# Written slots for the experts' steps, and early rows for the second place of every other block, in a graph attention and experts kernel

## The chip, the cores and the metric

The kernel runs on one core of a Trainium2 chip, in one launch. The time is the device time of that core in microseconds (us), as the median of several runs. A profile is one further execution, recorded by the hardware profiler.

## What is computed

A layer of a graph network and a feed-forward layer with experts, in float32. There are 30,000 nodes with 256 features and 510,000 edges, sorted by destination, each of one of 8 types. For each of the 8 types and 4 heads a node has a vector of 64 features:

```python
feat_all = jnp.einsum('ni,rhid->rnhd', inputs, conv_weights)      # inputs: layernorm(x)
feat_src_e = feat_all[edge_type, edge_src]
feat_dst_e = feat_all[edge_type, edge_dst]
el = jnp.sum(feat_src_e * attn_l[edge_type], axis=-1)
er = jnp.sum(feat_dst_e * attn_r[edge_type], axis=-1)
e = jax.nn.leaky_relu(el + er, negative_slope=LEAKY_SLOPE)
m = jax.ops.segment_max(e, edge_dst, num_segments=N_NODES)
ex = jnp.exp(e - m[edge_dst])
denom = jax.ops.segment_sum(ex, edge_dst, num_segments=N_NODES)
alpha = ex / denom[edge_dst]
h = jax.ops.segment_sum(alpha[..., None] * feat_src_e, edge_dst, num_segments=N_NODES)
```

Then x + h + bias goes through a layernorm, and the result is added to a shared network of three layers and to the best two of four experts, weighted by a softmax of the gates.

## The kernel before

There are two main stages. (A third part, a slow path for unusual inputs, runs zero times with these.)

**Features.** The 30,000 nodes are 235 tiles of 128. For each tile TensorE computes all types and heads at once in five groups of columns (`group`, the matmuls at L305). ACT and VectorE copy the results out of PSUM (L307), and SP's queue stores 128 x 8320 bytes to `feat` in HBM (`store`, L319). `feat` has one row of 260 numbers (1040 bytes) for each node and type: 4 heads of 64 features, and each head's part of the attention. GpSimd (POOL) adds the bias to x once for each four tiles (`residual`, L274). SP's loads, the copies and the matmuls run in an order written out by hand (`manual_schedule`); each engine executes its own queue in order.

Beside the tiles run generators, one step of which is put in after the third group of a tile and later also after the fifth (`aside`): `edge_records` writes an index record for each edge, and `places` makes the plan of each of the 252 blocks. A block is 16 places of 128 edges, one edge for each partition and place. The plan brings the edge with the smallest row number of a partition into place 0, with a `mark` that remembers where it stood. `places` works on batches of 12 blocks, in VectorE instructions with some copies on POOL.

Place 0 is thereby an early row: it lies in a tile that is finished well before the end of the stage. From tile 178 on, `first_rows` gathers these 252 rows of 128 partitions from the first three quarters of `feat` (L615, on POOL) and writes them to `stage` in HBM (L610, on SP).

**Edges.** The 252 blocks (and a last one of 18 places) are pipelined by hand. An iteration t of the loop has six chunks c, in each of which several blocks at different steps put their instructions into the queues:

- `load(t + 2)` and `gather(t + 1)` at c = 0. `gather` reads the early row from `stage` (SP, L931) and the other 15 places by one indirect DMA each (POOL, L933) into `ft`, a ring of four blocks.
- `dest_select`, `dest_expand` and `dest_pick` select the destination's part of the attention with one-hot matmuls (TensorE, L987) and VectorE (L998, L1000).
- `scores(t)` at c = 1 adds both parts, and calls `exchange`, which undoes the swap of places (VectorE, L1018, L1020, L1022), since the maximum over neighbours is taken by scans over the edges in order (L1033, L1034). `turn_ends`, `across`, `turn_back` carry the maximum across partitions. `softmax(t)` at c = 5 subtracts it (L1062 to L1065) and calls `exchange` again to bring the values back to the swapped places. `exps` is on ACT (L1071, L1072).
- `weigh` multiplies the gathered rows by the weights (VectorE, L1079), six pieces a block. `onehot` (ACT, L1010, L1011) makes the one-hot matrices with which `sums` adds the rows by destination (TensorE, L1086). `finish` divides (L1104 to L1107).
- When four blocks are finished, `residual_sum` makes the 22 steps of the experts (`Experts.steps`) for these 512 nodes and appends them to the list `todo`, of which one step is taken in each chunk, so in 22 chunks one after another of the next 24. Steps are matmuls with what follows on ACT or VectorE: `turn` (L742, L744), `layer` (L798, L799), `gates` (L750), `choose`, `weigh` (L835, L838), `last` (L851 to L857). What must come after a step's matmuls, such as VectorE's sum of the output (L857) and its store (`put`, L1097), waits in `late` for the start of the next chunk.

Of the kernel before, what the change touches and what calls it, by code (L numbers as in the profile page):

```python
# [10 lines left out]
F32 = mybir.dt.float32  # L11
# [34 lines left out]
WI, WD, WA, WP, W1, WT, WR = 0, U, 2 * U, 3 * U, 4 * U + 1, 6 * U + 3, 6 * U + 3 + U * 4  # L46
# [7 lines left out]
def kernel(  # L54
# [47 lines left out]
    stage = dram.tile([NBLK * P, H * HW], F32, name="stage")  # L102
# [119 lines left out]
    with ExitStack() as cx:  # L222
# [263 lines left out]
        BT = 3 * NT // 4  # L486
        count = {"ready": 0, "sent": 0}
        low = gp.tile([P, NBLK], I32, name="low")
        lowc = gp.tile([P, NBLK], I32, name="lowc")

        def places(cl):


            GB = 12
# [28 lines left out]
            yield  # L523
            done = None
            for k, (b0, n) in enumerate(batches):
# [4 lines left out]
                key = kp.tile([P, GB, U], F32, name="key", bufs=1)[:, :n]  # L530
                km = kp.tile([P, GB], F32, name="km", bufs=1)[:, :n]
                x = rc[:, :, :U, :3].rearrange("p b u f -> p b f u")
                mark = of[:, :, WA:WA + U]
                nc.vector.scalar_tensor_tensor(key, rc[:, :, :U, 0], float(U),
                                               iu[:, None, :].to_broadcast([P, n, U]), op0=ALU.mult, op1=ALU.add)
                nc.vector.tensor_reduce(km, key, AX.X, ALU.min)
                yield
                if done:
                    done()
                nc.vector.tensor_tensor(mark, key, km[:, :, None].to_broadcast([P, n, U]), op=ALU.is_equal)  # L540
                m3 = mark[:, :, None, :].to_broadcast([P, n, 3, U])
                t3 = kp.tile([P, GB, 3, U], F32, name="t3", bufs=1)[:, :n]
                nc.vector.tensor_mul(t3, x, m3)
                yield
                for f in range(3):
                    nc.vector.copy_predicated(x[:, :, f, 1:], o[:, :, WA + 1:WA + U],
                                              x[:, :, f, 0:1].to_broadcast([P, n, U - 1]))
                yield
                with nc.allow_low_precision(reason="integers below 2 ** 24"):
                    nc.vector.tensor_reduce(x[:, :, :, 0], t3, AX.X, ALU.add)  # L550
# [52 lines left out]

        def first_rows():

            n, kept = 4, []
            fp = cl.enter_context(tc.tile_pool(name="first", bufs=3))

            def keep(b0, m, fr):
# [795 lines left out]
```

## Time and profile before

| | us |
|---|---|
| median of 3 runs | 6651.61 |
| lowest and highest | 6647.99 and 6666.63 |
| the profiled execution | 8380.65 |
| its span, first to last instruction | 8379.0 |

The profiled execution is much longer than the runs without a profile. In the page of the profile, "busy" is the time in which an engine executes an instruction; in the row of a group, `x` is the number of instructions. "Idle before" is the time that the engine stood still before such instructions, with what ended most of it. The gathers are POOL's `DMA_INDIRECT`:

| group | count | busy us, mean ns of one |
|---|---|---|
| L933, gathers of the edge stage | 3798 | 3608.6, 950 |
| L615, gathers of the early rows | 252 | 240.6, 955 |
| L1086, TensorE's sums | 8100 | 2305.4, 421 |
| L1079, weighing on VectorE | 1518 | 1289.9, 850 |

In a timeline, each row has the start, the duration, the engine, the line, the operation with its tiles and shapes, how many instructions were merged into the row, and in brackets the idle time before with what ended it ("issue": nothing that the profile shows; "remote": a signal without a recorded sender).

### The profile page before, as it was taken

Reading aid. Unit: us, or ns where it says so; the run is one execution under the profiler, and the core shown is the slowest. Engines: PE = TensorE matmul, PEld = TensorE weight load, DVE = VectorE, ACT = ScalarE, POOL = GpSimd, SP = SyncE. Lnnn points to the kernel's source line nnn. Section 1 sums busy time; section 2 is a strip of 40 time slices with the busy share of each in tenths; the row PEclk is TensorE's granted clock in tenths of the full one; section 3 lists DMA queues with packets and bytes.
Section 4 is the critical chain, followed back from the end, with each engine's and each line's share of the span. In section 5 each row is a group of like instructions: output and inputs, shape, how many; then the busy total and the mean of one; then the engine's idle time right before and its main releaser. Section 6 shows DMA issues by size and latency. Waiting matters only on the chain. (4 is left out here: it accounts for less than half of the span.)

```text
span 8379.0 us, 96556 instructions
## 1 busy us (share of the span) xinstructions
PE 6330.2 (76%) x25254; PEld 3986.0 (48%) x25255; DVE 5381.4 (64%) x13882; ACT 3416.7 (41%) x9511; POOL 4073.5 (49%) x4327
## 2 busy tenths in 40 slices
PE   9999999956666767777666667777666777777667
PEld 5555555534444444444444444444444444444444
DVE  5557774447666666666666666666666666666665
ACT  2222222224444444444444444444444444444444
POOL 1101114665555555555555555555555555555552
PEclk9999999978888888888888888888888888888888
DMA  6657778964444444444444444444444444444441
GB/s 226 229 177 238 224 243 303 341 197 123 116 117 117 118 116 119 119 121 119 117 120 117 119 116 118 118 123 118 118 116 117 118 119 118 116 119 117 115 118 55
DMA packets 761457, 1209.52 MB, mean 144 GB/s; under 512 B 241638, under 2 KB 599789, under 8 KB 730685
## 3 DMA queue, kind: packets, MB, share of 16 engines
q1 hardware_dynamic: 565453, 663.56, 24.8%
q0 software_dynamic: 194400, 539.40, 23.3%
q8 instruction: 206, 3.38, 0.2%
q14 instruction: 358, 2.93, 0.1%
q10 hardware_dynamic: 1040, 0.26, 0.0%
HBM read 818.57 MB, written 384.23 MB: 144 GB/s over the span
## 5 line engine op out<-in xcount | busy, mean ns | idle before, releaser
L933 POOL DMA_INDIRECT ft<-feat,rk x3798 | 3608.6, 950 | 2919.9 <-PE po L1086 956.0
L1086 PE MATMUL po<-ft,oh 128*128 128x260 f32 x8100 | 2305.4, 421 | 286.3 <-DVE ho L1107 149.5
L1086 PEld LDWEIGHTS po<-ft,oh 128*128 128x128 f32 x8100 | 1565.4, 208 | 569.7 <-issue 292.4
L305 PE MATMUL ps<-w,xT 128*128 128x448 f32 (+1 forms) x4700 | 1712.6, 519 | 14.3 <-DVE xT L294 8.6
L1079 DVE TENSOR_TENSOR ft<-ft,p 128x768 f32<-128x768 f32 x1518 | 1289.9, 850 | 394.8 <-issue 184.1
L1010 ACT ACTIVATE oh<-icol,rk 128x128 f32<-128x128 f32 x4032 | 1329.1, 389 | 66.4 <-remote 45.5
L305 PEld LDWEIGHTS ps<-w,xT 128*128 128x128 f32 x4700 | 877.3, 191 | 704.9 <-issue 613.5
L798 PE MATMUL ph<-xT,w 128*128 128x512 f32 (+1 forms) x512 | 372.1, 859 | 961.8 <-issue 888.7
L307 ACT COPY fo<-ps 128x448 f32<-128x448 f32 (+1 forms) x711 | 377.3, 533 | 1087.4 <-PE ps L305 912.4
L998 DVE TENSOR_TENSOR ere<-pe,rk 128x384 f32<-128x384 f32 x1008 | 553.3, 549 | 373.4 <-remote 247.9
L1011 ACT ACTIVATE oh<-oh 128x384 f32<-128x384 f32 x1518 | 740.2, 488 | 49.4
L987 PEld LDWEIGHTS <-ohT 128*128 128x128 bf16 x4050 | 393.9, 158 | 548.8 <-issue 438.1
L798 PEld LDWEIGHTS ph<-xT,w 128*128 128x128 f32 x512 | 112.3, 260 | 1112.1 <-issue 952.5
L744 ACT COPY xT<-ph 128x512 f32<-128x512 f32 (+1 forms) x128 | 73.1, 572 | 1325.3 <-remote 1299.9
L1000 DVE TENSOR_REDUCE e<-ere 128x16 f32<-128x384 f32 (+1 forms) x1012 | 561.5, 555 | 34.8
L987 PE MATMUL pe<-erp,ohT 128*128 128x96 bf16 x4050 | 442.3, 236 | 113.3 <-DVE ohT L970 73.5
L798 PE MATMUL ph<-xT,v 128*128 128x512 f32 (+1 forms) x1024 | 500.2, 613 | 2.3 <-ACT h L799 1.5
L1062 DVE TENSOR_TENSOR c<-t,rk 128x128 f32<-128x128 f32 x252 | 71.8, 285 | 618.9 <-remote 582.0
L1071 ACT ACTIVATE p<-e 128x64 f32<-128x64 f32 (+1 forms) x253 | 70.4, 278 | 844.9 <-DVE e L1022 741.8
L307 DVE COPY fo<-ps 128x448 f32<-128x448 f32 (+1 forms) x464 | 242.3, 528 | 221.9 <-PE ps L305 194.2
L1040 PE MATMUL t<-ident,fb 128*4 128x128 f32 x253 | 70.8, 280 | 383.6 <-DVE fb L1033 196.7
L851 PE MATMUL pf<-w,h 128*128 128x256 f32 x506 | 203.2, 491 | 189.1 <-ACT wT L844 85.1
(206 smaller groups left out, 7422.2 us busy)
## 6 DMA issues: line engine op xcount, KB each, us to landing
feat<-fo SPq DMA_DIRECT2D x234, 1040.0 KB
dr<-dk_d SPq DMA_DIRECT2D x252, 516.0 KB
ft<-feat,rk POOLq DMA_INDIRECT x3798
stage<-fr SPq DMA_DIRECT2D x63, 520.0 KB
ft<-stage SPq DMA_DIRECT2D x252, 130.0 KB
xt<-xb_d SPq DMA_DIRECT2D x253, 128.0 KB
out_dram<-og SPq DMA_DIRECT2D x253, 128.0 KB
xb_d<-xb SPq DMA_DIRECT2D x58, 512.0 KB
```

Source lines behind the costliest of these rows:

```text
L305: nc.tensor.matmul(ps, t["xT"][:, k, :], w[:, k, c0:c1], start=k == 0, stop=k == 1)
L307: eng(t["fo"][:, h0:h1, :HD], ps[:, :n].rearrange("p (a d) -> p a d", d=HD))
L798: nc.tensor.matmul(ps[:, :self.w], lhs, rhs, start=i == 0, stop=i == len(pairs) - 1)
L851: nc.tensor.matmul(pf[:M], self.h2[:, tok], w3, start=True, stop=False)
L933: nc.gpsimd.indirect_dma_start(out=s.ft[:, u].rearrange("p h d -> p (h d)"), out_offset=None, in_=feat[:, :], in_offset=bass.IndirectOffse ...
L987: nc.tensor.matmul(pe[:, u - u0].rearrange("p f r -> p (f r)"), s.ov[:, u, :], s.erp.rearrange("n h k r -> n (h k r)"), start=True, stop=True)
L998: nc.vector.tensor_mul(ere, s.pe[:, :u1 - u0], s.th[:, u0:u1, None, :].to_broadcast([P, u1 - u0, H * 3, R]))
L1000: nc.vector.tensor_reduce(s.e[:, :, u0:u1].rearrange("p h u -> p u h"), ere.rearrange("p u (h k) r -> p u h (k r)", h=H), AX.X, ALU.add)
L1010: nc.scalar.activation(s.oh[:, u, :], icol, AF.Abs, bias=s.nd[:, u:u + 1])
L1011: nc.scalar.activation(s.oh[:, u0:u1], s.oh[:, u0:u1], AF.Relu, bias=1.0, scale=-1.0)
L1079: nc.vector.tensor_mul(fc, fc, pc[:, :, None].to_broadcast([P, (u1 - u0) * H, HD]))
L1086: nc.tensor.matmul(s.po.rearrange("n h d -> n (h d)"), s.oh[:, u, :], s.ft[:, u].rearrange("p h d -> p (h d)"), start=u == 0, stop=u == s. ...
```

## The change

Two things change.

1. In every other block (t even) the second place, too, gets an early row: of the remaining 15 places of each partition, the one with the smallest row number is swapped into place 1. So there are 252 + 126 = 378 early rows. `places` makes both swaps, `first_rows` gathers all 378 rows during the features, from tile 156 on, and `gather` reads one or two of them from the two tensors `stages`. How far into `feat` a gather may reach now depends on when it is issued (`rows_there`). The tensors hold three blocks' rows side by side (3120 bytes a partition), and are written three at a time. In the edge stage `exchange` is called for both places of such a block.

2. The 22 steps of the experts are no longer taken one after another. They have written slots (`SLOTS`), up to slot 27 of a group that starts every 24 chunks, so that the last four lie beside the first steps of the next group.

```diff
-WI, WD, WA, WP, W1, WT, WR = 0, U, 2 * U, 3 * U, 4 * U + 1, 6 * U + 3, 6 * U + 3 + U * 4
+WI, WD, WA, WP, W1, WT, WR = 0, U, 2 * U, 4 * U, 5 * U + 1, 7 * U + 3, 7 * U + 3 + U * 4
...
-    stage = dram.tile([NBLK * P, H * HW], F32, name="stage")
+    NS = 3
+    stages = [dram.tile([-(-n // NS), P, NS * H * HW], F32, name=f"stage{i}")
+              for i, n in enumerate((NBLK, (NBLK + 1) // 2))]
...
-        BT = 3 * NT // 4
+        NF = (NBLK, (NBLK + 1) // 2)
+        FIRST = NT * 2 // 3
+        RATE = 1.02 * sum(NF) / (NT - 1 - FIRST)
+        GB = 12
...
+        def rows_there(i, b0):
+            at = b0 - b0 % GB if i == 0 else NBLK + b0 - b0 % (GB // 2)
+            return min(NT - 2, int(FIRST + at / RATE) - 2) * P * R
...
             fetch(0)
-            yield
+            for _ in range(6):
+                yield
...
-                nc.vector.scalar_tensor_tensor(key, rc[:, :, :U, 0], float(U), ...)
-                nc.vector.tensor_reduce(km, key, AX.X, ALU.min)
+                nc.gpsimd.memset(o[:, :, WA + U:WA + 2 * U], 0)
+                for i in range(2):
+                    v = rc[:, ::i + 1, i:U]
+                    m, w = (n + i) // (i + 1), U - i
+                    x = v[:, :, :, :3].rearrange("p b u f -> p b f u")
...
+                    nc.vector.scalar_tensor_tensor(key, v[:, :, :, 0], float(U),
+                                                   iu[:, None, :w].to_broadcast([P, m, w]), op0=ALU.mult, op1=ALU.add)
+                    nc.vector.tensor_reduce(km, key, AX.X, ALU.min)
...
-                nc.gpsimd.tensor_copy(low[:, b0:b0 + n], rc[:, :, 0, 0])
-                nc.gpsimd.tensor_scalar_min(lowc[:, b0:b0 + n], rc[:, :, 0, 0], float(BT * P * R - 1))
+                for i, (c0, m, v) in enumerate(((b0, n, rc[:, :, 0, 0]), (b0 // 2, (n + 1) // 2, rc[:, ::2, 1, 0]))):
+                    most = rows_there(i, c0)
+                    nc.gpsimd.tensor_scalar_add(low[i][:, c0:c0 + m], v, float(-most))
+                    nc.gpsimd.tensor_scalar_min(lowc[i][:, c0:c0 + m], v, float(most - 1))
...
+            for i, n in enumerate(NF):
+                for b0 in range(0, n, NS):
+                    m = min(NS, n - b0)
+                    fr = fp.tile([P, NS, H * HW], F32, name="fr")
+                    for b in range(m):
+                        nc.gpsimd.indirect_dma_start(
+                            out=fr[:, b], out_offset=None, in_=feat[0:rows_there(i, b0 + b), :],
+                            in_offset=bass.IndirectOffsetOnAxis(ap=lowc[i][:, b0 + b:b0 + b + 1], axis=0))
...
-                    if m >= BT + 2:
-                        fetched = min(fetched + 1.03 * NBLK / ((NT - BT - 2) * NG), 3)
+                    if m >= FIRST:
+                        fetched = min(fetched + RATE / NG, 3)
...
+        SLOTS = (0, 1, 2, 4, 5, 7, 8, 9, 10, 11, 12, 13, 14, 15, 16, 18, 19, 21, 24, 25, 26, 27)
...
+                self.early = 2 - t % 2 if self.own else 0
...
-            if s.own:
-                nc.sync.dma_start(s.ft[:, 0].rearrange("p h d -> p (h d)"), stage[t * P:(t + 1) * P, :])
-            for u in range(1 if s.own else 0, s.u):
+            for i in range(s.early):
+                b = t >> i
+                f = b % NS * H * HW
+                nc.sync.dma_start(s.ft[:, i].rearrange("p h d -> p (h d)"), stages[i][b // NS, :, f:f + H * HW])
+            for u in range(s.early, s.u):
                 nc.gpsimd.indirect_dma_start(
...
-        def exchange(s, x):
-            if not s.own:
+        def exchange(s, x, i):
+            if i >= s.early:
                 return
-            m = wk.tile([P, H, U], F32, name="m", bufs=1)
-            nc.vector.tensor_mul(m, x, s.mark[:, None, :].to_broadcast([P, H, U]))
-            at = [P, H, U - 1]
-            nc.vector.copy_predicated(x[:, :, 1:], s.marki[:, None, 1:].to_broadcast(at),
-                                      x[:, :, 0:1].to_broadcast(at))
+            m = wk.tile([P, H, U], F32, name="m", bufs=1)[:, :, i:]
+            x = x[:, :, i:]
+            mark = s.marks[:, i, None, i:]
+            nc.vector.tensor_mul(m, x, mark.bitcast(F32).to_broadcast([P, H, U - i]))
+            at = [P, H, U - 1 - i]
+            nc.vector.copy_predicated(x[:, :, 1:], mark[:, :, 1:].to_broadcast(at), x[:, :, 0:1].to_broadcast(at))
             nc.vector.tensor_reduce(x[:, :, 0], m, AX.X, ALU.add)
...
-            exchange(s, s.e)
+            exchange(s, s.e, 1)
+            exchange(s, s.e, 0)
...
             nc.vector.tensor_sub(s.e, s.e, s.f)
-            exchange(s, s.e)
+            exchange(s, s.e, 0)
+            exchange(s, s.e, 1)
...
-                todo.extend(groups.pop(q).steps())
+                first = free[0] = max((t + 2) * NCH, free[0])
+                free[0] += T * NCH
+                for i, f in zip(Experts.SLOTS, groups.pop(q).steps()):
+                    plan.setdefault(first + i, []).insert(0, f)
...
-                    if todo:
-                        after = todo.pop(0)()
+                    for f in plan.pop(t * NCH + c, ()):
+                        after = f()
                         if after:
                             late.append(after)
```

## The prediction

> **What bounds the kernel now.** I read the page first, then windows by stage, then one group of four blocks in the timeline.
>
> ```profile
> span 8379.0 us, 96556 instructions
> ...
> PE 6330.2 (76%) x25254; PEld 3986.0 (48%) x25255; DVE 5381.4 (64%) x13882; ACT 3416.7 (41%) x9511; POOL 4073.5 (49%) x4327
> ```
>
> No engine looks full, and the profiled execution (8380.65 us) is 1729 us longer than the median of 6651.61 us. The timeline says where those 1729 us sit:
>
> ```profile
> 4101.01 0.58 ACT L744 COPY xT<-ph 128x512 f32<-128x512 f32 x1 [21.73 <-remote]
> ```
>
> ACT copies a transpose that TensorE finished near 4081 us only at 4101. "Remote" means that the signal it waited for did not come with any recorded instruction; VectorE waits in the same way there. The list of waits has this one 63 times, 1299.9 us in all, once for each group of four blocks. 1729 us over 63 groups is 27 us each, so I take these late signals, and smaller ones beside them, as part of the profiled execution, and work with each engine's own durations instead of its idle time. This is a choice, and the largest uncertainty of what follows.
>
> ```profile
> 1162.00:1313.00 151.00, 151.00 (x455) 81.90 (x454) 97.70 (x267) 39.16 (x84) 20.40 (x26) 1.00 0.76 243
> 1313.00:1750.00 437.00, 429.29 (x1282) 232.43 (x1280) 189.62 (x594) 109.21 (x233) 273.13 (x266) 0.99 0.95 331
> ...
> 2500.00:8000.00 5500.00, 3877.71 (x16860) 2565.55 (x16859) 3670.57 (x9302) 2489.57 (x7178) 3024.64 (x3183) 0.85 0.42 118
> ```
>
> Columns: stretch, length, busy time of PE, PE's loads, DVE, ACT, POOL, then clock, DMA share, GB/s. Two stages: features to about 1750 us, where PE is the bound and, in the last 437 us, the DMA engines are nearly full too; then 253 blocks of edges with no engine full.
>
> ```profile
> L1104 DVE TENSOR_SCALAR den<-po x253: 154/155/165, 1851.9 to 8323.0; 128x4 f32<-128x4 f32 x127
> ```
>
> One such instruction ends each block: 6471.1 us over 252 blocks is 25.7 us a block in the profile. For the median: 6651.6 less 1750 (features), some 50 (filling the ring) and 56 (8323 to the end) leaves about 4796 us, 19.0 us a block.
>
> What fills 19.0 us? POOL first:
>
> ```profile
> 4071.14 0.95 POOL L933 DMA_INDIRECT ft<-feat,rk  x1 [0.30 <-DVE ft L1079]
> 4072.39 0.95 POOL L933 DMA_INDIRECT ft<-feat,rk  x1 [0.30 <-issue]
> ```
>
> One gather every 1.25 us, 15 a block: 18.8 us. VectorE next: 3670.57 us busy in 5500 us, which is 214.2 blocks, so 17.1 us and 43 instructions a block. But short dependent instructions leave gaps that no other work can fill:
>
> ```profile
> 4054.47 0.23 DVE L1028 SCALAR_TENSOR_TENSOR e<-e 128x64 f32<-128x64 f32 x1
> 4054.72 0.23 DVE L1018 TENSOR_TENSOR m<-e,rk 128x64 f32<-128x64 f32 x1
> 4054.99 0.23 DVE L1020 COPY_PREDICATED e<-rk,e 128x60 f32<-128x60 int32 x1
> 4055.25 0.22 DVE L1022 TENSOR_REDUCE e<-m 128x4 f32<-128x64 f32 x1
> 4055.51 0.29 DVE L1033 TENSOR_TENSOR_SCAN fb<-penf,e 128x64 f32<-128x64 f32 x1
> ```
>
> Starts lie 0.26 us apart for 0.22 to 0.23 us of work; some 20 such gaps of 0.04 us make 0.8 us. And in each block VectorE stands idle between the softmax and the first weighing, for ACT's exponential and copy:
>
> ```profile
> 4070.17 0.95 DVE L1079 TENSOR_TENSOR ft<-ft,p 128x768 f32<-128x768 f32 x1 [0.71 <-ACT ft L1072]
> ```
>
> 17.1 + 0.8 + 0.7 = 18.6 us. So POOL (18.8) and VectorE (18.6) both lie within 2% of the pace of 19.0. PE's 3877.71 us are 18.1 us a block at a clock of 0.85, so less at full clock.
>
> **What the Trainium skill says.** "Perfetto Trace Analysis", section "DMA Instruction — SWDGE (GPSIMD)": a gather's recorded end is when the descriptors are written, not when the rows land. The trace agrees: 0.95 us each, whether the DMA share is 0.42 or 1.0. So POOL's time depends on the count of gathers. The same page, "Optimizing Scalar/DVE Operations": a VectorE instruction on SBUF carries about 60 ns of access overhead, and its profiled latency about twice that; 64 elements at 0.23 us show that small instructions cost mostly overhead here. "DMA: Bandwidth & Descriptors", section "Where 436 GB/s comes from": about 358 GB/s of HBM for a core; the trace agrees, with 357 and 365 GB/s at a DMA share of 1.03 and 1.01 in stretches of the features.
>
> **The change part by part.**
>
> *Removed from POOL's edge stage:* 126 gathers (one in every other block) of 1.2535 us (0.95 + 0.30): 157.9 us. POOL's work falls to 18.2 us a block. If POOL alone sets the pace, this is all gained.
>
> *Added to VectorE's edge stage:* the blocks with two early rows call exchange twice more, once in scores and once in softmax: 3 instructions each, 0.26 us from start to start: 1.58 us a block, 199 us over 126 blocks. The tiles of 60 and 56 elements instead of 64 and 60 save a few ns. VectorE goes to 18.6 + 0.79 = 19.4 us a block on average, above today's 19.0. Nothing else of its work goes away: steps of the experts only move. Beside what can it lie? Only VectorE's waits for others: 19.0 - 18.6 = 0.4 us a block, 100 us. Waits for gathers among them vanish as POOL gets ahead; those for PE and ACT do not. Bounds: all 199 us on the path, or 99 us. The pieces are chains at fixed places (scores, before TensorE's turn of the ends; softmax, before ACT's exponentials), and the queue behind each is the weighing that TensorE's sums wait for. I take 30 us absorbed: +169 us.
>
> *The experts' slots.* The same 22 steps, in 24 to 28 slots. TensorE's four matmuls of a 512-wide layer take 1.88 us (4013.78 to 4015.66), the 16 of the gates 1.84 us. Before, the group's second block has gates, one shared layer and four expert layers: 11.2 us on top of the sums. After, that block has 9.4 us, the third about 9.2 us, the fourth hardly any, and the four last steps fall into the next group's first block. This smooths TensorE's peak, and moves VectorE's four output sums (0.42 us each) into a block without the second exchange; but it leaves TensorE's heavy third block beside VectorE's lightest. Nothing here shows either effect alone: -50 to +60 us (a quarter us a block either way); I take 0. New group's steps come ahead of the old group's last in the shared slots, with tiles of their own; the copies of x1 alternate between two buffers, so no new wait on a buffer.
>
> *The features.* 378 gathers instead of 252, from tile 156 of 235 on at 4.94 a tile, instead of from tile 178 at 4.55. POOL: a quad of tiles lasts 29.2 us (7.31 a tile) and now has 20 gathers (25.1), one residual sum (2.36) and, while the block plans are still being made, about 2.9 us of their copies: 30.3 us. That is 1 us a quad late, some 11 quads: 12 us of lag, made up by nothing. DMA: the stretch before the gathers moves 243 GB/s, plans included. 4.94 gathers a tile read and write back 133 KB each, 180 GB/s. With the plans a fifth slower that is about 414 GB/s for 44 tiles (322 us), against some 358 GB/s: 18 MB too much, 50 us of transfer; afterwards 185 + 180 = 365 GB/s lets it recover nothing. The write-back in rows of 3120 instead of 1040 bytes may spare some. SP's queue is passed by more write-backs, each waiting for its gathers, and feature stores stand behind them; six tiles of lead hide about 44 us. What is left appears as a late start of the edge stage. Bounds 0 and +50 us; I take +25. VectorE's second ordering in the plans (11 pauses a batch instead of 9) lies beside PE-bound matmuls: nothing, as VectorE is busy 98 of 151 us there. More expert weights arrive later, but far ahead of their use.
>
> *The start of the edge stage:* the ring of four blocks fills with two gathers less: -2.5 us. SP issues one more small read in every other block: nothing, it runs ahead.
>
> Sum: 169 + 0 + 25 - 2 = +192 us. On the profiled execution, 8380.65 + 192 = 8573 us; on the median, 6651.6 + 192, rounded: **6840 us**.
>
> **The rivals.**
> (B) POOL alone sets the pace, and VectorE's true need is a whole us a block below what the profile gives (its gaps stretched by the recording, as TensorE's signals were). For it: POOL's 18.8 is the larger of the two, and a ring of four blocks can keep POOL running without a pause. Against: VectorE's durations look the same in quiet and crowded stretches. Then 6651.6 - 158 + 25 + 20 (VectorE takes over in the two-row blocks) = 6540 us. The point from which it decides: VectorE below about 18 us a block before the change.
> (C) Both fall together: gain and cost cancel, 6600 to 6700 us, about 6650.
> (D) The features also stretch: the DMA excess of 50 us and POOL's lag stop TensorE as well; 6840 + 50 = 6890 us.
> That the early rows don't get fetched in time is excluded by the order of POOL's queue: of 378 gathers 7 stand behind the last residual sum, against 10 before.
>
> **How the numbers follow.** VectorE's pace (my forecast) 0.52, B 0.27, C 0.12, D 0.09. My forecast's own range is 6740 to 6910 us: 99 to 199 us of exchange, ±55 of slots and 0 to 50 of features, not all at one end. The range for all is 6515 to 6920 us, which leaves out less than half of B's lower side and a few parts of D. A measurement here can tell 0.3% (20 us) from nothing: faster takes B and a third of C (0.31), within 0.3% a third of C (0.04), slower the rest (0.65).
>
> **What would show it.** Right: in the changed profile, VectorE's busy time in the edge stage grows by about 170 us and three more of its instructions stand in a row in every other block, while POOL's gaps at L933's successor grow. Wrong: shorter total with VectorE waiting for gathers less than before; or a shorter wait at the first weighing, which would mean that the slots freed VectorE. For the features: DMA share near 1.0 from about 1165 us, and the first gather of the edge stage later than 1750 us.

## The result, and the profile after

The changed kernel takes 7131.75 us (median of 4 runs, 7127.65 to 7135.18) against 6652.67 us before: a ratio of 1.0716 (95% interval 1.0698 to 1.0735), 479 us slower. The forecast had the direction, but 192 us for the size. On two chips every run of the kernel before took 8350 to 8480 us, like the profiled execution in the prediction, and on the others about 6655 us, so each run below is compared with the kernel before on its own chip, and the runs beside 6655 us carry the argument.

The changed kernel's profiled run (7135.18 us) agrees with its median. Its page, with the busy times, the slices of PE, and three groups of instructions (busy time, mean ns, idle time before and what ended most of it):

```profile
span 7133.5 us, 97813 instructions
...
PE 6186.2 (87%) x25254; PEld 3969.0 (56%) x25255; DVE 5576.9 (78%) x14808; ACT 3428.9 (48%) x9511; POOL 4094.6 (57%) x4390
...
PE   9999999779688888888888888888888888888888
...
L972 POOL DMA_INDIRECT ft<-feat,rk x3672 | 3479.9, 948 | 1668.4 <-PE pe L1026 536.2
...
L1121 DVE TENSOR_TENSOR ft<-ft,p 128x768 f32<-128x768 f32 x1518 | 1288.6, 849 | 364.3 <-ACT ft L1114 364.3
...
L644 POOL DMA_INDIRECT fr<-feat,lowc x378 | 372.5, 985 | 297.6 <-DMA stage<-fr 185.4
```

Three things stand here. POOL idles 1668 us ahead of the edge gathers. Some 1100 us of that are the 0.30 us between any two gathers, but with 15 gathers a block (f_features below) it is 1228 us in all: POOL waits more than before, so the time of the 126 gathers it was spared is not gained. VectorE waits 364 us at the first weighing (L1121) for ScalarE's copy: 1.44 us a block, where 0.71 us was the wait seen before. And the PE row dips in its eighth and ninth slices (about 1250 to 1600 us), inside the features, where TensorE was full before.

Where the two stages stand, by single lines (L972 is the edge gather, L933 before; L1147 ends a block, L1104 before):

```profile
L972 POOL DMA_INDIRECT ft<-feat,rk x3672: 940/946/1132, 1890.2 to 7022.5; - x194
```

```profile
L1147 DVE TENSOR_SCALAR den<-po x253: 152/154/163, 1939.8 to 7074.8; 128x4 f32<-128x4 f32 x127
```

The edge gathers of x_exch2, a run below with the features of before:

```profile
L936 POOL DMA_INDIRECT ft<-feat,rk x3798: 940/946/1197, 1742.8 to 6681.1; - x200
```

The first edge gather comes at 1890.2 us. In the runs that leave the features alone (x_exch2, s_slots2, b_hot2) it comes at 1742.8, 1744.4 and 1742.2: the features lost 147 us. The blocks then run at (7074.8 - 1939.8) / 252 = 20.38 us. f_features below, which has the old edge stage, runs at 19.10 us; 1.28 us times 252 is 323 us. 147 + 323 = 470 of the 479 us.

**The features.** Windows of the changed kernel, then of x_exch2 (columns as in the prediction):

```profile
1200.00:1300.00 100.00, 82.12 (x232) 43.36 (x230) 52.82 (x140) 18.32 (x41) 55.22 (x64) 0.91 0.85 276
1300.00:1400.00 100.00, 79.42 (x223) 42.36 (x224) 59.25 (x158) 19.19 (x42) 59.65 (x65) 0.86 0.82 262
1400.00:1500.00 100.00, 62.70 (x173) 32.58 (x172) 44.60 (x109) 14.38 (x32) 59.84 (x70) 0.81 0.84 280
1500.00:1600.00 100.00, 73.06 (x208) 38.94 (x207) 37.88 (x119) 17.35 (x37) 57.05 (x62) 0.86 1.00 305
1600.00:1700.00 100.00, 100.00 (x303) 54.55 (x302) 47.64 (x144) 25.99 (x55) 61.92 (x62) 1.00 0.92 327
```

```profile
1300.00:1400.00 100.00, 100.00 (x302) 54.28 (x301) 49.62 (x144) 26.01 (x56) 52.81 (x51) 1.00 0.88 301
1400.00:1500.00 100.00, 100.00 (x301) 54.29 (x300) 42.91 (x137) 25.70 (x54) 67.36 (x67) 1.00 1.01 359
```

From 1200 to 1600 us TensorE loses 103 us. Up to 1500 us no engine fills that hole: VectorE is about half idle, POOL is busy 55 to 60%, the DMA share is 0.82 to 0.85, and from 1300 us on the DMA engines move less than in x_exch2. That is a queue standing behind something, not a full resource; only from 1500 to 1600 us, at a DMA share of 1.00, do the windows leave it open. The changed kernel's timeline shows one such stop:

```profile
1419.84 0.95 POOL L644 DMA_INDIRECT fr<-feat,lowc  x1 [0.30 <-DMA stage<-fr]
1420.79 0.36 POOL L594 COPY rko<-a1k 128x204 f32<-128x204 f32 x1
1421.10 0.35 POOL L595 COPY rko<-a2k 128x204 f32<-128x204 f32 x1
1421.49 0.96 DVE L601 TENSOR_TENSOR rko<-rcb,it 128x768 bf16<-128x768 int32 x1 [21.68 <-POOL rko L595]
1422.36 0.42 DVE L297 COPY xT<-ptr 128x256 f32<-128x256 f32 x1
...
1422.83 1.86 PE L308 MATMUL ps<-w,xT 128*128 128x448 f32 x2 [16.37 <-DVE xT L297]
```

Read it from below. TensorE waits 16.37 us for the transposed rows xT. VectorE's copy of them stands in its queue behind L601, the last step of a plan, which has waited 21.68 us for POOL's two copies into the same tile, and those stand behind gathers in POOL's queue. The Trainium skill, "TensorE: Matmul & The Clock Gate", section "Architectural detail: the array is 16× 32×32, not 1× 128×128", gives VectorE's queue as strictly first in, first out, and GpSimdE's too for each of its cores; the trace agrees, since a copy of 0.42 us waited behind an instruction that it has nothing to do with. The gathers themselves stand still as well: 185 us in all, until earlier rows are copied out of their buffers (L644 above).

The last step of the plans and the early gathers, before (L579, L615) and in the changed kernel (L601, L644):

```profile
L579 DVE TENSOR_TENSOR rko<-rcb,it x42: 944/951/2981, 604.1 to 1264.8; 128x768 bf16<-128x768 int32 x42
```

```profile
L615 POOL DMA_INDIRECT fr<-feat,lowc x252: 943/949/1190, 1313.2 to 1731.3; - x126
```

```profile
L601 DVE TENSOR_TENSOR rko<-rcb,it x42: 941/950/959, 618.3 to 1540.7; 128x768 bf16<-128x768 int32 x42
```

```profile
L644 POOL DMA_INDIRECT fr<-feat,lowc x378: 940/946/1682, 1142.7 to 1874.3; - x189
```

Before, the gathers begin when the plans are through. Now they begin at 1143 us, and the plans run until 1541 us. The change has moved both ends: the gathers start 170 us earlier, and each of the 21 batches of plans has eleven pauses in place of nine. At the old pace of a pause the plans would end near 1426 us (618 + 661 x 11/9, an estimate from these lines).

**The edges.** ScalarE's queue in a third block of a group in the changed kernel, with VectorE's last instruction of the exchange (L1062) and the weighing that waits:

```profile
4017.38 0.69 ACT L860 ACTIVATE a<-ph,c 128x512 f32<-128x512 f32 x1
4017.96 0.61 ACT L864 COPY wide<-wt 128x512 f32<-128x512 f32 x1
4018.18 0.22 DVE L1062 TENSOR_REDUCE e<-m 128x4 f32<-128x64 f32 x1
4018.47 0.99 ACT L1049 ACTIVATE oh<-icol,rk 128x128 f32<-128x128 f32 x3
4019.49 0.53 ACT L1050 ACTIVATE oh<-oh 128x384 f32<-128x384 f32 x1
4019.92 0.27 ACT L1113 ACTIVATE p<-e 128x64 f32<-128x64 f32 x1
4020.22 0.28 ACT L1114 COPY ft<-p 128x64 f32<-128x64 f32 x1
...
4020.54 0.95 DVE L1121 TENSOR_TENSOR ft<-ft,p 128x768 f32<-128x768 f32 x1 [2.13 <-ACT ft L1114]
```

The scores e are ready at 4018.40 (4018.18 + 0.22), but the exponential (L1113) starts at 4019.92: ScalarE is still at the one-hots of the block's fifth chunk, and these came late because slot 16 has put the second half of experts2 (L860, L864) into that chunk. In the old list the 17th step lay there, the second weigh of a group, which has no ScalarE instruction. The group's first block waits as long, for another step:

```profile
4057.43 0.58 ACT L779 COPY xT<-ph 128x512 f32<-128x512 f32 x1 [6.80 <-PE ph L777]
4057.91 0.98 ACT L1049 ACTIVATE oh<-icol,rk 128x128 f32<-128x128 f32 x3
4058.93 0.53 ACT L1050 ACTIVATE oh<-oh 128x384 f32<-128x384 f32 x1
4059.48 1.28 ACT L1113 ACT_TABLE_LOAD   x1
4060.77 0.28 ACT L1113 ACTIVATE p<-e 128x64 f32<-128x64 f32 x1
```

Slot 4 is the first turn; its copy (L779) waits for TensorE, the one-hots follow, and behind them the exponential needs a table load of 1.28 us, because the group's square root came between. L1121 waits 2.22 us there. In f_features the same load is done (4076.57 to 4077.85 us in its profile) before the scores are ready (4078.17).

VectorE's account of four consecutive blocks makes the edge stage comparable. It is taken from the timelines, from one end of a block to the next, as a mean over 55 groups of four; idle is the sum of gaps over 0.1 us between VectorE's instructions:

```
kernel         work, us   idle, us   four blocks, us
f_features       71.75       4.72        76.46   (the old edge stage)
x_exch2          74.76       3.76        78.51
s_slots2         71.60       6.91        78.49
changed          74.67       7.12        81.78
k_hot            74.82       4.48        79.31
b_slothot        71.71       3.82        75.53
b_hot2           71.93       6.85        78.79
```

There are 63 groups. The change adds 2.9 us of work and 2.4 us of idle time to each.

### The profile page after: what moved, and what is told of

Same layout as the page of the kernel before. It is cut to its first block, busy times and chain, and to the rows that moved or that the text cites. A ratio compares the mean times of both kernels' runs of the same rounds, so it can differ in the third digit from the quotient of the medians.

```text
span 7133.5 us, 97813 instructions
## 1 busy us (share of the span) xinstructions
PE 6186.2 (87%) x25254; PEld 3969.0 (56%) x25255; DVE 5576.9 (78%) x14808; ACT 3428.9 (48%) x9511; POOL 4094.6 (57%) x4390
## 5 line engine op out<-in xcount | busy, mean ns | idle before, releaser
L972 POOL DMA_INDIRECT ft<-feat,rk x3672 | 3479.9, 948 | 1668.4 <-PE pe L1026 536.2
L1128 PE MATMUL po<-ft,oh 128*128 128x260 f32 x8100 | 2372.8, 431 | 400.9 <-DVE ho L1150 213.5
L1128 PEld LDWEIGHTS po<-ft,oh 128*128 128x128 f32 x8100 | 1588.6, 211 | 820.2 <-ACT ends L994 398.3
L308 PE MATMUL ps<-w,xT 128*128 128x448 f32 (+1 forms) x4700 | 1730.8, 524 | 107.0 <-DVE xT L297 104.8
L1121 DVE TENSOR_TENSOR ft<-ft,p 128x768 f32<-128x768 f32 x1518 | 1288.6, 849 | 364.3 <-ACT ft L1114 364.3
L644 POOL DMA_INDIRECT fr<-feat,lowc x378 | 372.5, 985 | 297.6 <-DMA stage<-fr 185.4
L1026 PE MATMUL pe<-erp,ohT 128*128 128x96 bf16 x4050 | 424.9, 230 | 52.8 <-DVE ohT L1009 52.1
L834 ACT ACTIVATE h<-ph,b 128x512 f32<-128x512 f32 x192 | 130.9, 682 | 449.3 <-PE ph L833 446.5
L297 DVE COPY xT<-ptr 128x256 f32<-128x256 f32 x229 | 97.2, 424 | 319.1 <-PE ptr L295 318.1
L1009 DVE TENSOR_SCALAR ohT<-dr,rowid 128x2064 bf16<-128x2064 int16 (+1 forms) x253 | 324.0, 1281 | 18.4 <-DMA feat<-fo 18.4
L833 PE MATMUL ph<-xT,w 128*128 128x512 f32 (+1 forms) x512 | 311.7, 744 | 0.2 <-ACT xT L779 0.2
L779 ACT COPY xT<-ph 128x512 f32<-128x512 f32 (+1 forms) x128 | 74.6, 584 | 462.1 <-PE ph L777 462.1
```

Source lines behind the costliest of these rows:

```text
L308: nc.tensor.matmul(ps, t["xT"][:, k, :], w[:, k, c0:c1], start=k == 0, stop=k == 1)
L644: nc.gpsimd.indirect_dma_start(out=fr[:, b], out_offset=None, in_=feat[0:rows_there(i, b0 + b), :], in_offset=bass.IndirectOffsetOnAxis(ap ...
L833: nc.tensor.matmul(ps[:, :self.w], lhs, rhs, start=i == 0, stop=i == len(pairs) - 1)
L972: nc.gpsimd.indirect_dma_start(out=s.ft[:, u].rearrange("p h d -> p (h d)"), out_offset=None, in_=feat[:, :], in_offset=bass.IndirectOffse ...
L1026: nc.tensor.matmul(pe[:, u - u0].rearrange("p f r -> p (f r)"), s.ov[:, u, :], s.erp.rearrange("n h k r -> n (h k r)"), start=True, stop=True)
L1121: nc.vector.tensor_mul(fc, fc, pc[:, :, None].to_broadcast([P, (u1 - u0) * H, HD]))
```

## The experiments

Part by part first. The first four runs were made on a chip where the kernel before takes 8370.42 us.

**The slots alone** on the kernel before (the part of the diff with SLOTS, plan and free).

> The kernel before with only the written slots for the experts' steps; the early rows and the features stay as they were. The whole change costs 479 us, of which the two profiles put 140 us before the first gather of the edge stage (1750.5 against 1890.2 us) and so 339 us into the edge stage. Theory 1 (VectorE sets the edge stage's pace, the second exchange costs its full 199 us): the slots cost the rest, 140 us, so about 6790 us. Theory 2 (POOL set the pace; exchange and saved gathers cancel; the slots are what costs): 339 us, about 6990 us. A third value, at or below 6650 us, would mean that the slots help and that the second row costs more than it shows. The late signals at the copy of the transposes, 1299.9 us in the profile before, should be gone from this profile if the slots removed them.

Measured: 8307.89 us, ratio 0.9928 (0.9909 to 0.9947). In its profile ACT's waits of 21 us at the copy of the transposes are gone, but VectorE stands still for 870 us in all at the gates (L766, 64 times), mostly for TensorE: with the new order the long waits are at another step.

**Everything but the slots:** the changed kernel with the old list of steps.

```diff
-                for i, f in zip(Experts.SLOTS, groups.pop(q).steps()):
-                    plan.setdefault(first + i, []).insert(0, f)
+                todo.extend(groups.pop(q).steps())
```

> The changed kernel with the experts' steps taken one after another as before: second early rows, their gathers in the features and the second exchange, no slots. Theory 1: 6652 + 140 (features) + 199 (exchange) = about 6990 us. Theory 2: 6652 + 140 and nothing for the edge stage, about 6790 us. If the parts add up, this and the run with slots alone sum to the 479 us of the whole change.

Measured: 8452.85 us, ratio 1.0106 (1.0090 to 1.0123).

**The second exchange alone:** in every even block of the kernel before, three more instructions in scores and three in softmax, with a mark that swaps a row with itself.

```diff
+            if s.own and t % 2 == 0:
+                exchange_same(s, s.e)
```

> The kernel before with the second exchange alone: in every other block three more VectorE instructions in scores and three in softmax, of the shapes of the change, with a mark that swaps nothing. Theory 1 (VectorE sets the pace): 6652 + 199 = 6850 us, at least 6750. Theory 2 (POOL sets the pace and VectorE has about a us a block to spare): within 30 us of 6652.

Measured: 8442.52 us, ratio 1.0083 (1.0061 to 1.0105).

**One gather less in even blocks**, its place filled by SP with the first place's row.

```diff
-            for u in range(1 if s.own else 0, s.u):
+            early = 2 - t % 2 if s.own else 0
+            if early == 2:
+                nc.sync.dma_start(s.ft[:, 1].rearrange("p h d -> p (h d)"), stage[t * P:(t + 1) * P, :])
+            for u in range(early, s.u):
```

> The kernel before with one gather less in every other block: the second place is filled by SP from the rows already staged for the first place, so that its rows are wrong there; no second exchange, no gathers more in the features. Theory 1 (VectorE sets the pace): 6652 us, within 40. Theory 2 (POOL sets the pace): 126 gathers of 1.2535 us less, 6652 - 158 = 6495 us.

Measured: 8262.86 us, ratio 0.9868 (0.9832 to 0.9905).

On this chip the changes are all within 1.4% of the kernel before. I take it that TensorE's late signals set the pace of each group there, which no run separates; what the parts cost beside 6655 us these four runs don't tell, and for the spared gathers alone no other run tells it. They do tell that the late signals are no effect of profiling alone: all seven runs of the kernel before lie between 8352 and 8379 us, while the profiled executions beside 6655 us, such as f_features (6817.04 us), have no wait named "remote".

The next four runs have the kernel before at 6656.08 us (7 runs).

**The changed kernel itself.**

> The changed kernel itself, beside the kernel before on the same chip. Theory (the late TensorE signals of before are a state of the chip that the new order of steps does not meet): about 7130 us whatever the kernel before shows, so slower by 7% where that takes 6650 and faster by some 15% where it takes 8370. Rival (every kernel on such a chip carries them): about 8700 us beside 8370.

Measured: 7133.36 us, ratio 1.0722 (1.0704 to 1.0740). On this chip both times repeat, so it does not decide between theory and rival. Two runs below do: n_lag1 and y_hotearly have the changed kernel's slots and second exchange, and take 8404 and 8375 us beside 8454 us. So the new order of steps meets the late signals too, against the theory.

**The features alone:** the changed kernel's plans and 378 early gathers, with the edge stage and the list of steps of before. The second swap is made in the plans and not undone, so the kernel leaves out a part of the computation. One of its edits:

```diff
-                self.early = 2 - t % 2 if self.own else 0
+                self.early = 1 if self.own else 0
```

> The features and plans of the changed kernel (378 early gathers, both orderings in each plan), the steps one after the other as before and only the first early row used: 15 gathers and one exchange in each own block. The second exchange and its swap are left out. Theory: the first edge gather comes at about 1890 us as in the changed kernel, and the whole is 140 us slower than the kernel before (about 6790 beside 6650, or 8510 beside 8370). Rival (the loss of 140 us of the features belongs to the profiled execution or is made up at the edges): within 30 us of the kernel before.

Measured: 6815.25 us, ratio 1.0237 (1.0220 to 1.0255), 159 us over the kernel before; the first edge gather is at 1891.9 us. So the features' loss is real, appears whole in the total, and belongs to the feature stage by itself.

**The second exchange alone**, again.

> The kernel before with a second exchange in every other block that swaps a row with itself, once more, to be read if the kernel before takes about 6650 us on this chip. Theory (VectorE paces the edges): 126 exchanges of 1.58 us each, +150 to +200 us. Rival (POOL's 15 gathers of 1.25 us pace the block and VectorE has slack): under +60 us. Where the kernel before takes 8370 us it should repeat the +72 us already measured.

Measured: 6788.70 us, ratio 1.0203 (1.0186 to 1.0220), +133 us. VectorE paces; but of 199 us of added instructions 66 are absorbed. By what, the table and the waits tell. VectorE's waits from 2000 to 6700 us, f_features and then x_exch2 (us in all, times, longest):

```profile
DVE og L892 <- PE pf L889: 91.0, 138, 1.6
DVE den L1146 <- PE po L1128: 22.4, 59, 0.5
```

```profile
DVE og L860 <- PE pf L857: 51.0, 126, 1.6
```

The idle time falls from 4.72 to 3.76 us a group, 60 us over 63 groups: VectorE waited for TensorE's last layers of the experts, and an exchange that makes it later shortens that wait. POOL is close behind VectorE all the same: between 2100 and 6400 us of f_features its gathers pause for more than 0.35 us only 31 times, 57 us in all (183 us in x_exch2).

**The plans' POOL operations on VectorE:** eight lines (L542, L577 to L579, L583, L585, L594, L595), of which one is shown.

```diff
-                nc.gpsimd.tensor_copy(of[:, :, W1:W1 + UW], a1)
+                nc.vector.tensor_copy(of[:, :, W1:W1 + UW], a1)
```

> The changed kernel with the nine small POOL operations of each plan on VectorE, so that nothing VectorE waits for in a plan stands behind a gather in POOL's queue. Theory (during the features POOL's gathers hold back the plan's copies, these VectorE, and VectorE's copy of the transposed rows TensorE): the first edge gather moves from 1890 back to about 1770 us and the whole gains 90 to 130 us on the changed kernel. Rival (the 126 gathers and 126 more row copies take the DMA engines from the features' loads): no change, within 20 us.

Measured: 7122.84 us, against 7133.36: 11 us gained, first edge gather 1875.0 us. That is the value of the rival, though the run does not test the rival's reason. The wait went, and another took its place. VectorE's longest wait from 1100 to 1900 us in this kernel:

```profile
DVE a_st L138 <- DMA xg<-in_x_dram: 127.5, 13, 19.0
```

No wait for POOL's copies into rko is left (117.6 us in the changed kernel); in its place the wait for the next tiles' input rows has grown to 127.5 us, from 43.7 us. Those rows are loaded by SP, whose queue stands 352 us at the copies of gathered rows. So the wait that the trace names is real, but the loss does not hang on it alone: my expectation failed.

Four runs with the kernel before at 6656.59 us:

**The plans earlier:** up to three steps of the plans in a feature tile, not two.

```diff
-                    if g == 2 or g == 4 and len(side) < 3:
+                    if g == 2 or g in (0, 4) and len(side) < 3:
```

> The changed kernel with the plans stepped up to three times in a feature tile, not two, so that they end before or soon after the first early gather. Theory (the loss of the features comes of gathers and plans running side by side: POOL's copies for the plans stand behind gathers, SP's loads of rows behind the copies of gathered rows): TensorE stays busy through the features but for VectorE's load, the first edge gather moves from about 1885 to 1760-1800 us, and the whole gains 80 to 125 us. Rival (the DMA engines are the bound of the stretch, with or without plans): within 30 us of the changed kernel.

Measured: 7059.31 us, ratio 1.0603 (1.0585 to 1.0620), 74 us less than the changed kernel (7133.36 us, on a chip with the same kernel before within 1 us). The windows of p_early, and its edge gathers:

```profile
1100.00:1200.00 100.00, 90.00 (x264) 47.61 (x263) 65.72 (x175) 22.23 (x50) 26.90 (x36) 0.97 0.96 281
1200.00:1300.00 100.00, 100.00 (x304) 54.37 (x303) 49.57 (x143) 25.61 (x54) 65.35 (x66) 1.00 0.94 333
1300.00:1400.00 100.00, 100.00 (x302) 54.42 (x301) 45.45 (x140) 25.36 (x54) 66.33 (x64) 1.00 0.93 328
1400.00:1500.00 100.00, 92.35 (x268) 49.27 (x268) 40.20 (x123) 22.11 (x49) 65.00 (x65) 0.97 0.93 331
```

```profile
L972 POOL DMA_INDIRECT ft<-feat,rk x3672: 940/946/1202, 1810.2 to 6946.9; - x194
```

With the plans over by 1160 us, TensorE is full from 1200 to 1400 us and over 92% in the window that had 62.70 us. The first edge gather comes 80 us earlier. So about half of the features' loss is plans and gathers running side by side; the other 67 us (1810 against 1743) have another cause.

**The one-hots of the fifth chunk after the exponentials,** on the changed kernel.

```diff
                     if c == 5:
                         at(softmax, t)
                         at(exps, t)
+                        at(onehot, t, 4)
...
-                    at(onehot, t, c)
+                    if c != 4:
+                        at(onehot, t, c)
```

> The changed kernel with one order changed on ScalarE: the one-hots of the fifth chunk of a block (L1049, L1050) come after the block's exponentials (L1113, L1114), not ahead of them. Theory (the slots put the groups' ScalarE copies into the fifth chunk of every second block, so that the exponentials come 1.4 us late there and VectorE, which paces the edges, waits 2.13 and 2.22 us instead of 0.73 us at L1121): the waits fall to 0.73 us in all blocks, and the whole gains (1.40 + 1.49) us x 63 = 180 us on the changed kernel, to about 6950 us. Rival (VectorE only waits there for something that would be late anyway, one-hots or TensorE): a gain under 50 us.

Measured: 6974.52 us, ratio 1.0481 (1.0463 to 1.0498), 159 us less than the changed kernel. The group on its page:

```profile
L1121 DVE TENSOR_TENSOR ft<-ft,p 128x768 f32<-128x768 f32 x1518 | 1289.5, 850 | 189.6 <-ACT ft L1114 189.6
```

364.3 us have become 189.6, 0.75 us a block: the waits of 2.13 and 2.22 us are gone. 175 us of wait gave 159 us of time.

**The slots alone**, again.

> The kernel before with the experts' steps in the written slots alone, to be read if the kernel before takes about 6650 us on this chip. Theory (the slots' ScalarE copies delay the exponentials; POOL's 15 gathers of 1.25 us hide a part, as they already bound one block at 18.8 us): slower, by 60 to 180 us. Rival (the slots cost nothing, and the remainder of the changed kernel's loss is a meeting of exchange and slots): within 40 us of the kernel before.

Measured: 6785.66 us, ratio 1.0193 (1.0176 to 1.0210), +129 us. The same wait, without the change's other parts:

```profile
L1081 DVE TENSOR_TENSOR ft<-ft,p 128x768 f32<-128x768 f32 x1518 | 1289.5, 850 | 367.8 <-ACT ft L1074 367.8
```

The rest of the slots' idle time is smaller than before: the waits for the last layers, which absorbed a part of the exchange, are gone. So exchange and slots together cost more than 133 + 129: in the table the changed kernel stands 3.29 us a group over s_slots2, 207 us in 63 groups, all of the second exchange's 199 us.

**Slots and late one-hots on the kernel before.**

> The kernel before with the slots, and with the one-hots of the fifth chunk after the exponentials on ScalarE. Theory: the slots' delay is taken away and VectorE has about 71.8 us of work and 3.0 us of waits in four blocks, against 76.5 us for four blocks in the kernel before, so the bound is POOL's 15 gathers at 18.8 us: 0 to 80 us faster than the kernel before. Rival (the late one-hots hold TensorE's sums in turn): slower than the kernel before.

Measured: 6606.50 us, ratio 0.9925 (0.9909 to 0.9942): faster than both kernels. Its pace is (6545.2 - 1793.6) / 252 = 18.86 us, against 18.80 us for POOL's 15 gathers. Two rows of POOL's queue:

```profile
3000.51 0.95 POOL L935 DMA_INDIRECT ft<-feat,rk  x1 [0.30 <-DVE ft L1081]
3001.76 0.94 POOL L935 DMA_INDIRECT ft<-feat,rk  x1 [0.30 <-PE pf L856]
```

Of the 3423 gathers between 2100 and 6400 us none comes after a longer pause than 0.31 us. So here POOL is the bound: in the kernel before the two engines were nearly tied, and the 50 us gained are about what POOL's pauses (57 us in f_features) left to gain.

Three runs have the kernel before at 8453.64 us. **Copies of the gathered rows one at a time, five gathers late,** on p_early:

```diff
-    NS = 3
+    NS = 1
...
-                        if b == NS // 2 and kept:
-                            keep(*kept.pop())
+                        if b == NS // 2 and len(kept) > 5:
+                            keep(*kept.pop(0))
```

> The changed kernel with the plans stepped faster (as in p_early) and the gathered rows copied out one row at a time, each only after five later gathers were issued, from 11 one-row buffers. Theory (SP waits for gathers at the head of its queue, and the next tile's rows are loaded late for it): SP's waits for fr at the row copy (some 350 us in the changed kernel) fall below 50 us, VectorE's waits for xg (84.6 us in p_early) go, and 40 to 60 us are gained on p_early, to about 7010 us. Rival (the DMA engines, over 90% busy there, are the bound): within 20 us of p_early at 7059 us.

Measured: 8404.24 us, ratio 0.9942 (0.9921 to 0.9963). The total can't be set beside 7059 us. For the feature stage there is y_hotearly below, on the same chip and with p_early's plans: its first edge gather is at 1806.1 us, p_early's at 1810.2. SP's wait at the row copy from 1100 to 1900 us, p_early and then n_lag1, and a window of n_lag1:

```profile
SPq L637 <- DMA fr<-feat,lowc: 388.3, 126, 8.2
```

```profile
SPq L637 <- DMA fr<-feat,lowc: 15.4, 17, 2.6
```

```profile
1400.00:1500.00 100.00, 98.10 (x295) 52.74 (x294) 42.77 (x136) 24.20 (x53) 68.14 (x68) 1.00 1.01 355
1500.00:1600.00 100.00, 88.24 (x252) 46.57 (x251) 38.45 (x117) 21.16 (x47) 61.59 (x61) 0.95 0.89 307
```

SP hardly waits any more, and VectorE's wait for the input rows has fallen from 84.6 to 2.2 us, but the first edge gather is at 1817.4 us, not earlier. One of VectorE's new waits there, from 1100 to 1850 us:

```profile
DVE xT L297 <- remote: 45.2, 6, 12.1
```

These are late signals inside the features (y_hotearly has 10.4 us of them, in one wait), and they may have taken what SP's queue gave back. So SP's part in the remaining 67 us stays open. The other candidate is the DMA engines, 89 to 101% busy at 307 to 355 GB/s in the windows above; the Trainium skill ("DMA: Bandwidth & Descriptors", section "Where 436 GB/s comes from") puts the limit of a core's transfers with HBM near 358. But from 1400 to 1700 us x_exch2 moves 341 to 359 GB/s with TensorE full, while p_early moves 325 to 331 with TensorE busy 92 to 94%. No run took bytes away, so the cause of the 67 us isn't shown.

**Both edits on the changed kernel** (p_early's and k_hot's), and **the late one-hots alone on the kernel before**, on that chip:

> The changed kernel with both edits: the plans stepped faster and the fifth chunk's one-hots after the exponentials. Theory (two separate places, features and edges): the gains of 73 and 158 us add, about 6900 us, still some 245 us or 3.7% over the kernel before. Rival (one of the two is made up by the other): over 6960 us.

> The kernel before with only the fifth chunk's one-hots after the exponentials. Theory (in the old order of steps VectorE waits 0.73 us for the exponentials in every block already, the least there is): within 15 us of the kernel before, so that the 50 us of b_slothot are the slots' gain, once their delay is taken away. Rival (the one-hots' order alone gains them): 30 to 60 us faster.

Measured: 8374.60 us, ratio 0.9899 (0.9869 to 0.9929), and 8491.08 us, ratio 1.0044 (1.0033 to 1.0055). Both were repeated beside a kernel before of 6661.48 us.

> The changed kernel with faster plans and late one-hots, to be read where the kernel before takes about 6650 us. Theory (independent places): about 6900 us, 3.7% over the kernel before. Rival (one is made up by the other): over 6960 us.

Measured: 6892.92 us, ratio 1.0353 (1.0323 to 1.0382). 7133.36 less 74 and 159 is 6900: the two gains add, as those of independent places do.

> The kernel before with only the fifth chunk's one-hots after the exponentials, to be read where the kernel before takes about 6650 us. Theory (VectorE already waits the least there): within 15 us of the kernel before. Rival (the one-hots' order alone gains what b_slothot gained): 30 to 60 us faster.

> The slots with late one-hots on the kernel before, beside b_hot2 on one chip. Theory: 50 us faster than the kernel before where that takes about 6650 us; where it takes about 8400, some 0.7% faster, as the slots alone were there.

Measured: 6805.29 us for the late one-hots alone, ratio 1.0221 (1.0192 to 1.0250), 144 us *slower*; and 6609.91 us with the slots, 0.9928 (0.9899 to 0.9956), as in the first run of it. Neither theory nor rival had the first. VectorE's waits from 2000 us on in b_hot2:

```profile
DVE og L857 <- PE pf L854: 208.6, 209, 2.8
DVE ft L1079 <- ACT ft L1072: 172.3, 239, 1.0
```

In the old list the four last layers (L854) follow one another, a step a chunk, in one block of the four. All of the loss lies in that block: it takes 22.1 us on average, with TensorE busy for 20.4, against 19.8 us in f_features, and the other three differ by 0.1 us at most. With the one-hots late, TensorE's sums come late, these layers behind them, and VectorE's output sums wait (91.0 us in f_features, 208.6 here). The slots spread those four steps and this wait goes. That TensorE was held by the one-hots I infer from the order; no run separates it. The gain of 50 us belongs to neither edit alone: each by itself costs 129 and 144 us.

## Why the prediction was wrong

The direction and the pace-setting engine were right. Two terms of the sum failed: the slots, taken as 0 and measured at 129 us, and the features, taken as 25 us and measured at 147 us (159 us in the total). Point by point, by its own steps:

- *"VectorE paces", POOL's 158 us not gained:* right. The 17.1 + 0.8 us of VectorE's work in a block stand in f_features as 71.75 / 4 = 17.9 us. POOL's idle time at the edge gathers grew from 1228 us in f_features to 1668 us, VectorE's work in a group by 2.9 us, 184 us in all, beside the foreseen 170. Rival B is out: the second exchange costs 133 us alone, and with the slots all of it appears in the time.
- *"30 us absorbed: +169 us" for the exchange:* near. Alone it costs 133 us (66 absorbed), on top of the slots some 200.
- *The slots, "-50 to +60 us; I take 0":* this term failed. They cost 129 us alone. I weighed TensorE's matmuls of each step and VectorE's output sums, but not ScalarE's share (1.3 us for L860 and L864 in one block, a late copy and a table load in another), nor what is queued behind it: one-hots, exponential, and VectorE's first weighing. The sign to look for was in the prediction's own list ("a shorter wait at the first weighing"); the wait doubled.
- *The features, "Bounds 0 and +50 us", +25:* this is the larger miss, 147 us. The prediction did put gathers and plans side by side, for 44 tiles, but it priced POOL's time (12 us of lag), the bytes (50 us) and VectorE's time ("VectorE's second ordering in the plans lies beside PE-bound matmuls: nothing"), and no waits. The overlap laid two streams of work into three queues that the next tiles share (POOL, SP, and VectorE behind both), and 80 us went when p_early took it away. The other 67 us are not explained. That they are near the 50 us of transfer is no proof: nothing here shows that bytes are their cause.
- *The late signals as part of the profiled execution:* wrong as a reason, since they go with the chip and the profiled executions beside 6655 us have none; as the median was used, the number survived.

The sum of the forecast, 169 + 0 + 25, reads 133 + 129 + 159 in single runs, 421 us of 479, and the rest, 58 us, is mostly the cover that the slots take from the exchange.

## What to carry to other kernels

When work is started earlier, list every queue it enters and what now stands behind it there, for waits in a queue can cost more than the work that was priced; removing the one wait that the trace names may only show the next. When steps are moved into slots, price their share on each engine, also the one that is half idle: what counts is which instruction stands behind them and who waits for it. Two edits that each lose can gain together where one takes away the wait that the other one makes, so try them in pairs before dropping them.

## What the runs showed that was not expected

Late TensorE signals of some 20 us, once per four blocks, come or stay away by chip: the same kernel before took 8352 to 8478 us on two chips and 6639 to 6679 us on the others. On the slower ones, changes worth 2% elsewhere moved the time by less than 1%, the slots even the other way (62 us faster there, 129 us slower beside 6655 us). What causes the late signals no run tells. And placing three one-hots and their closing instruction (1.5 us of ScalarE) behind an exponential moved the time by +144, -159 or -179 us (6785.66 to 6606.50), according to the order of the experts' steps.
